# Softmax weights turned on VectorE in four batches of the last cross attention and two of the last self attention, the context staged through the output buffer, and a shorter look-ahead for keys

## The chip, the cores and the metric

The kernel runs on one core of a Trainium2 chip, in fp32. The metric is the device time of one execution in microseconds (us), smaller is better: 1604.43 us is the median of three runs (1602.59 to 1607.76). About 0.3% (5 us) is what a measurement of this kernel can tell from no change.

The engines by the profile's names: PE (matrix multiply; PEld is its weight load), DVE (VectorE), ACT (ScalarE), POOL (GpSimd) and SP (the queue from which nearly all DMAs are issued, in the order of the program).

## The reference, cut to what matters

Four transformer blocks follow each other on x of 8 batches x 112 rows x 256 columns. All of them read the same context of 8 x 375 x 192. Every attention has 16 heads, of 64 columns in blocks L0, L1 and L2 and of 16 in block L3.

```python
x = self_attn(ln(x)) + x ; x = cross_attn(ln(x), ctx) + x ; x = geglu_ff(ln(x)) + x    # L0: stages 0, 1, 2
x = self_attn(ln(x)) + x ; x = cross_attn(ln(x), ctx) + x ; x = geglu_ff(ln(x)) + x    # L1: stages 3, 4, 5
x = x + cross_attn(ln(x), ctx)                                                         # L2: stage 6
x = x + causal_self_attn(ln(x)) ; x = x + cross_attn(ln(x), ctx) ; x = x + mlp(ln(x))  # L3: stages 7, 8, 9
# attention: w = softmax(q k^T / sqrt(dh)) over keys; out = w v; per batch and head 112 x 112 or 112 x 375 weights
```

## The kernel before, in words

All of x, the normalised and transposed input `hT`, the transposed context (`ctxA`, `ctxB`) and the attention output `oT` ([128, 8, 896], the "output buffer") stay in SBUF. Queries, keys and values live in one `arena`; weight matrices pass through a ring `wpool` of six slots, rows of biases through a ring of two.

Attention is cut into 176 *steps* (`add_step`): one batch with 8 heads in a self attention (2 steps a batch), one batch with 4 heads in a cross attention (4 steps a batch). The steps of stage 7 are woven between those of stages 6 and 8 (dictionary `after`). I number steps from 0 in that order: stage 6 begins at step 96, stage 8 at step 138, its batch 4 at step 158. A step has these parts.

- S (`emit_s`): the scores q k^T on PE (L1079) into PSUM, then the softmax. With 64-column heads DVE finds the row maxima (L1030), ACT takes exp with a row sum (L1036), POOL multiplies by the reciprocal (L1043). With 16-column heads (stages 7 and 8) one DVE operation adds the mask, negates, writes the masked scores to SBUF and leaves the maximum (L1012), ACT takes exp (L1020), and the division is done later on the output (`emit_norm`, `emit_scale`).
- The weights must then stand with keys on partitions. There are two ways. An *unturned* step transposes each 112 x 128 block on PE (T, L1109) and DVE or ACT copies four at a time out of PSUM (L1116, L1119, L355). A *turned* step transposes 32 x 32 blocks on DVE (`flip`, L1057), writes four strips to DRAM (`send`, L1063) and reads them back in the final layout (`fetch`, L980): the bounce through DRAM exchanges the 32-row strips. Two write tiles and two read tiles in `stage` serve all turned steps in turn; the fetch of a step waits for the PV of the turned step two before it.
- PV (`emit_pv`, L1142): weights times values on PE; the result is copied into `oT`.

`TURN(st, b, g)` says which steps are turned: in stage 7 batches 0 to 4, in stage 8 none, in stages 0, 1, 3, 4 and 6 nearly all.

Everything else is an `Item` with a cost, a due time in steps (`deadline`) and what it needs: query, key and value projections (L715, L756, L833/L842, L867/L876, L908/L917), output products with the next layer norm (L681), transposes of the normalised rows (L649) and of the context (L939), feed-forward. A planner (`Plan`) emits the program once: the loop over steps at the end of the kernel places S up to `lead(s)` steps ahead of PV (two, or up to four where turned steps follow each other) and fills in items by due time. Keys and values of a cross attention are *jobs*, opened by `open_jobs` when their due time is within a limit; before, the limit is `i + 1.5 + lead(...)`, so 3.5 to 5.5 steps after step i. Items that make queries, keys or values in the pending list are held back until `ahead` = 7 steps before they are due. The order so made is fixed; at run time each engine and the SP queue go through their own part of it in order.

The context is read by three loads into the weight ring (`add_ctx`: batches 0 to 2, 3 to 5, 6 and 7) and transposed on PE batch by batch (`add_context_transposes`, L939); batches 2 to 7 are due during stage 1, one every four steps. Each transposed batch needs one more DMA (`ctxB` to `ctxB`).

```python
fetches.append((s, dram))                                  # send: four DMAs stage -> DRAM, then
while fetches and turned[fetches[0][0]] < emptied[0] + 2 and free_of(fetches[0][0]): ...   # fetch: one DMA back
plan.open_jobs(1 if i + 1 >= first_of(8, 0) or i + 2 in woven else 2, i + 1.5 + lead(min(nxt, hi - 1)), seg)
```

## Time and profile before

| what | value |
|---|---|
| median of three runs | 1604.43 us |
| the profiled execution: its time / span of its instructions | 1604.4 us / 1602.6 us |
| PE, DVE, ACT, POOL busy | 95%, 55%, 45%, 34% of the span |
| granted TensorE clock | 0.985 |
| DMA moved, mean rate | 212.49 MB, 133 GB/s |
| sends and fetches | 488 and 122 DMAs, for 122 turned steps |
| stage 8 begins (scores of step 138) / its batch 4 (step 158) | 1372.9 us / 1469.6 us |

The page lists busy time by engine; since matmuls are pipelined and their ends are modelled, a busy PE is not PE at its peak. How fast PE takes matmuls is read from where they start. The list of windows gives busy time of all engines, the granted clock and DMA for a stretch; the chain of waits follows the work that ended last back in time.

### The profile page before, as it was taken

The page shows a single profiled execution, that of the slowest core. Times are in us where ns is not written, and L with a number is a line of the kernel's source. Part 1 is how long each engine was busy: PE and PEld are TensorE (multiplying, and loading weights), DVE is VectorE, ACT ScalarE, POOL GpSimd, SP SyncE. Part 2 cuts the span into 40 slices and gives each one's busy share as a digit, 9 for nine tenths or more (in the row PEclk, how much of TensorE's full clock was granted, in tenths as well). Part 3 has the DMA queues.
Part 4 walks back from the last instruction along what each step waited for, and adds up shares of the span by engine and source line. Part 5 has one row for each costly group of instructions (what it writes and reads, how often), then busy time and mean ns, then how long its engine had stood idle before and what let it go on. Part 6 is the DMA issues. An engine that isn't in the chain of part 4 may idle for free.

```text
span 1602.6 us, 28310 instructions
## 1 busy us (share of the span) xinstructions
PE 1530.4 (95%) x10452; PEld 1035.4 (65%) x10452; DVE 886.4 (55%) x2029; ACT 723.4 (45%) x2359; POOL 537.2 (34%) x787
## 2 busy tenths in 40 slices
PE   9998999999999989999999999989999997999999
PEld 8776656665567876666565556655566545666667
DVE  3664555566442265565655542455656766577762
ACT  3452435444332444444443351234445545587772
POOL 1333434444320223354334230433434336212210
PEclk9999999999999999999999999999999999899999
DMA  6165464766601056556575712045467667300000
GB/s 179 39 206 153 140 215 149 236 188 177 191 30 53 24 145 198 145 158 213 172 204 158 208 46 77 2 125 178 159 194 197 189 178 222 126 2 2 2 2 23
DMA packets 128305, 212.49 MB, mean 133 GB/s; under 512 B 11287, under 2 KB 112295, under 8 KB 128167
## 3 DMA queue, kind: packets, MB, share of 16 engines
q1 hardware_dynamic: 127927, 210.52, 44.5%
q8 instruction: 82, 1.34, 0.3%
q14 instruction: 56, 0.46, 0.1%
q10 hardware_dynamic: 240, 0.17, 0.0%
HBM read 122.45 MB, written 87.43 MB: 131 GB/s over the span
## 4 chain that ended last, share of the span: by engine, by line
PE 73%; DVE 9%; ACT 6%; DMA 5%; issue 3%; POOL 3%; SPq 1%; DVEq 0%; ACTq 0%; POOLq 0%
PE mm L681 12%; PE mm L715 10%; PE s L1079 8%; PE mm L1142 8%; PE mm L867 6%; PE mm L833 6%; PE mm L1384 6%; PE mm L842 4%; PE mm L876 4%; DVE stage L1057 3%; ACT pr L1036 3%; DMA stage<-b 3%; PE mm L1109 2%; DMA b<-stage 2%; POOL pr L1043 2%
## 5 line engine op out<-in xcount | busy, mean ns | idle before, releaser
L1043 POOL TENSOR_TENSOR pr<-pr,rinv 128x750 f32<-128x750 f32 (+3 forms) x224 | 327.7, 1474 | 342.6 <-DVE rinv L1041 342.0
L1036 ACT ACTIVATE pr<-s,nm 128x375 f32<-128x375 f32 (+3 forms) x640 | 302.3, 493 | 268.6 <-DVE nm L1030 213.5
L1057 DVE STREAM_TRANSPOSE stage<-pr 128x768 f32<-128x768 f32 (+2 forms) x218 | 206.9, 970 | 71.3 <-POOL pr L1043 62.7
L1079 PE MATMUL s<-arena 64*128 64x375 f32 (+6 forms) x1792 | 218.9, 403 | 16.4 <-ACT pr L1036 8.0
L1030 DVE TENSOR_REDUCE nm<-s 128x2 f32<-128x750 f32 (+3 forms) x224 | 205.6, 949 | 33.9 <-PE s L1079 32.2
L355 ACT COPY arena<-mm 128x375 f32<-128x375 f32 (+5 forms) x186 | 96.5, 520 | 274.8 <-PE mm L842 125.9
L1142 PE MATMUL mm<-stage,arena 128*64 128x112 f32 (+5 forms) x3840 | 189.9, 268 | 16.9 <-DMA stage<-b 11.5
L1142 PEld LDWEIGHTS mm<-stage,arena 128*64 128x64 f32 (+5 forms) x3840 | 168.8, 134 | 55.7 <-issue 18.9
L363 DVE COPY arena<-mm 128x375 f32<-128x375 f32 (+5 forms) x186 | 109.1, 594 | 158.9 <-PE mm L876 71.2
L1079 PEld LDWEIGHTS s<-arena 64*128 64x128 f32 (+3 forms) x1792 | 122.8, 184 | 101.3 <-issue 33.5
L1020 ACT ACTIVATE pr<-pr,nm 112x375 f32<-112x375 f32 (+2 forms) x256 | 124.7, 492 | 26.9 <-DVE nm L1012 26.7
L1036 ACT ACTIVATION_READ_ACCUMULATOR pr<-s,nm 128x1 f32 (+1 forms) x640 | 135.4, 212 | 0.0
L611 POOL TENSOR_TENSOR rs<-ve,mhalf 128x1 f32<-128x1 f32 x70 | 39.5, 564 | 212.1 <-DVE ve L609 212.0
L1041 DVE RECIPROCAL rinv<-sums 128x2 f32<-128x2 f32 (+3 forms) x224 | 37.6, 168 | 127.7 <-ACT pr L1036 127.1
L1002 POOL MEMSET pr<- 128x9 f32 (+1 forms) x218 | 23.0, 108 | 233.5 <-DVE stage L1057 205.3
L833 PE MATMUL mm<-ctxA,L_xattn_Wk 128*128 128x375 f32 x256 | 92.3, 488 | 6.4 <-ACT arena L351 2.5
L867 PE MATMUL mm<-L_xattn_Wv,ctxA 128*128 128x512 f32 (+1 forms) x192 | 93.7, 615 | 0.9 <-DVE x L685 0.5
L715 PE MATMUL mm<-hT,L_xattn_Wq 128*128 128x224 f32 x384 | 82.7, 361 | 4.2 <-DVE arena L363 2.1
L1109 PEld LDWEIGHTS mm<-ident,pr 112*128 112x128 f32 (+2 forms) x600 | 66.8, 151 | 30.3 <-issue 14.2
L1109 PE MATMUL mm<-ident,pr 112*128 112x112 f32 (+2 forms) x600 | 78.9, 266 | 4.3 <-ACT pr L1020 3.1
L685 DVE TENSOR_TENSOR x<-mm,x 128x256 f32<-128x256 f32 x70 | 29.4, 420 | 94.9 <-PE mm L681 94.3
L681 PE MATMUL mm<-L_xattn_Wo,oT 128*128 128x256 f32 x336 | 79.3, 391 | 0.8 <-ACT oT L355 0.8
(138 smaller groups left out, 2252.1 us busy)
## 6 DMA issues: line engine op xcount, KB each, us to landing
b<-stage SPq DMA_DIRECT2D x344, 192.0 KB, 3.9
stage<-b SPq DMA_DIRECT2D x86, 768.0 KB, 5.9
b<-stage SPq DMA_DIRECT2D x144, 128.0 KB, 3.6
stage<-b SPq DMA_DIRECT2D x36, 512.0 KB, 4.6
L_xattn_Wo<-in_L_xattn_Wo_dram SPq DMA_DIRECT2D x3, 1024.0 KB, 14.9
L_xattn_w_ff<-in_L_xattn_w_ff_dram SPq DMA_DIRECT2D x3, 1024.0 KB, 6.7
L_xattn_Wv<-in_L_xattn_Wv_dram SPq DMA_DIRECT2D x4, 512.0 KB, 7.3
L_xattn_Wq<-in_L_xattn_Wq_dram SPq DMA_DIRECT2D x2, 1024.0 KB
```

Source lines behind the costliest of these rows:

```text
L681: nc.tensor.matmul(ps[:, :D], lhsT=oT[:, c, t * P : (t + 1) * P], rhs=got[wv or w][:, c, :], start=(c == 0), stop=(c == n - 1),)
L715: nc.tensor.matmul(ps[:, i * 2 * T : (i + 1) * 2 * T], lhsT=got[w][:, k, m * P : (m + 1) * P], rhs=hT[:, k, lo:hi], start=(k == 0), stop=( ...
L833: nc.tensor.matmul(ps[:, :S], lhsT=got[wv][:, (2 * u + i) * P : (2 * u + i + 1) * P], rhs=ctxA[:, cols], start=True, stop=False,)
L867: nc.tensor.matmul(ps[: KCH[c][1], :], lhsT=lhs(ctxA, slice(0, KA), c), rhs=got[w][:, hf * 512 : (hf + 1) * 512], start=True, stop=False,)
L1020: return nc.scalar.activation(pr, pr, AF.Exp, bias=nm, scale=-1.0, accum_out=bsums[(st, b)][:, h : h + 1])
L1030: nc.vector.tensor_reduce(nm[:, :, :ns], sv, AX.X, ALU.max, negate=True)
L1036: nc.scalar.activation(pr[:, bk, sl, :], sv[:, bk, sl, :], AF.Exp, bias=nm[:, bk, sl : sl + 1], accum_out=sums[:, bk, sl : sl + 1],)
L1043: nc.gpsimd.tensor_tensor(pr, pr, rinv[:, :, :ns].unsqueeze(3).to_broadcast([rows, 2, ns, nk]), ALU.mult)
L1057: nc.vector.transpose(dst, src)
L1079: nc.tensor.matmul(tiles[i][:, n % 2, (n // 2) * nk : (n // 2 + 1) * nk], lhsT=qap(h), rhs=kap(h), start=True, stop=True,)
L1109: nc.tensor.transpose(pt[:kl, m * T : (m + 1) * T], cell[h][:, c * P : c * P + kl], ident[:T, :T])
L1142: nc.tensor.matmul(po[p0 : p0 + dp, blk * T : (blk + 1) * T], lhsT=got[vk][:kl, hv * dp : (hv + 1) * dp], rhs=wt, start=(c == 0 and par(h) ...
```

## The change

- Stage 8 becomes a turned stage: batches 0 to 3 turn their weights on DVE (16 steps); its queries are laid out in 32-row strips, and its due times move two steps earlier, as for the other turned stages.
- Stage 7: batches 5 and 6 are turned too (four steps), so 0 to 6 are.
- The context: batches 0 to 2 still go through the weight ring, in one load of 9 chunks; the other 15 chunks are loaded into columns 448 to 831 of `oT` by two DMAs that need no ring slot. All eight batches are due in stage 0 (3.5 + b/2). The PVs of steps 8 and 9 (batch 4 of stage 0, the first to write the part of `oT` with context in it) are placed after all context transposes.
- Key and value jobs are opened when due within 2.5 steps, instead of 3.5 to 5.5; `ahead` is 6 instead of 7.
- The mask of the context is kept on 128 partitions instead of 112, for turned steps.

Counted in the two programs: 224 transposes (L1109) fewer on PE; 56 copies of them out of PSUM fewer (35 on ACT, 21 on DVE); 40 DVE transposes more (32 of 128 x 768, 8 of 128 x 512); 80 sends and 20 fetches more on SP (64 and 16 of a cross step, 16 and 4 of a self step); 40 small memsets more on POOL for the columns that pad the weights, and 8 for the gaps in the queries. The number of exps, maxima, scores and PVs stays.

```diff
--- before.py
+++ after.py
@@ -27,7 +27,7 @@
 NQ, QR = 4, 28
 LEAD = 4
 TAIL = 6
-TURNED = (0, 1, 3, 4, 6, 7)
+TURNED = (0, 1, 3, 4, 6, 7, 8)
 NWT = 8
 NEG = -1.0e30
 EPS = 1e-5
@@ -95,7 +95,7 @@
         self.pool = {r: deque() for r in rings}
         self.refs, self.maker, self.ev = {}, {}, {}
         self.pending, self.loads, self.jobs, self.opened = [], deque(), [], []
-        self.now, self.step, self.ahead = 0.0, 0, 7
+        self.now, self.step, self.ahead = 0.0, 0, 6
 
     def add(self, it, filler=True):
         self.items[it.key] = it
@@ -500,13 +500,17 @@
         key = ("w", "ctx", i)
 
         def fn():
-            t = wpool.tile([CH, len(bs) * 3, DC], F32, tag="w", name="cn")
-            nc.sync.dma_start(
-                t, a["ctx_768"][bs[0] : bs[-1] + 1].rearrange("b (c p) d -> p (b c) d", p=CH)
-            )
-            got[key] = t
-
-        plan.add_load(Item(("load", key), 0, fn, makes=[key]))
+            src = a["ctx_768"].rearrange("b (c p) d -> p (b c) d", p=CH)
+            if i:
+                nc.sync.dma_start(oT[:CH, :, 448:640], src[:, 9:17, :])
+                nc.sync.dma_start(oT[:CH, 0:7, 640:832], src[:, 17:24, :])
+                got[("c", i)] = lambda n: oT[:CH, (n - 9) % 8, 448 + 192 * ((n - 9) // 8) :][:, :DC]
+                return
+            t = wpool.tile([CH, 9, DC], F32, tag="w", name="cn")
+            nc.sync.dma_start(t, src[:, 0:9, :])
+            got[("c", i)] = lambda n: t[:, n, :]
+
+        plan.add_load(Item(("load", key), 0, fn, makes=[] if i else [key]))
 
     def add_last_self(key, name):
 
@@ -581,14 +585,14 @@
         key = ("w", "cm")
 
         def place():
-            got[key] = wpool.tile([T, B, S], BF16, tag="w", name="cm")
+            got[key] = wpool.tile([P, B, S], BF16, tag="w", name="cm")
 
         plan.add_load(Item(("load", key), 0, place, makes=[key]))
         for b in range(B):
 
             def ctx_mask(b=b):
                 c = B * T + b * S
-                nc.gpsimd.tensor_scalar_mul(got[key][:, b, :], got[src][:T, c : c + S], NEG)
+                nc.gpsimd.tensor_scalar_mul(got[key][:, b, :], got[src][:, c : c + S], NEG)
 
             plan.add(Item(("mask", b), 0, ctx_mask, first_of(7, 0) - 6 + 0.5 * b, uses=[src, key], seg=SEG[6]))
 
@@ -928,22 +932,22 @@
 
     def add_context_transposes(deadline):
         for b in range(B):
-            key = ("w", "ctx", b // 3)
-
-            def fn(b=b, key=key):
-                cn = got[key]
+            key = ("w", "ctx", int(b > 2))
+
+            def fn(b=b):
+                cn = got[("c", int(b > 2))]
                 cols = slice(b * S, (b + 1) * S)
                 for k0, kl, dst in ((0, KA, ctxA), (KA, KB, ctxB)):
                     pc = mm_tile()
                     for c in range(3):
                         nc.tensor.transpose(
                             pc[:kl, c * CH : (c + 1) * CH],
-                            cn[:, (b % 3) * 3 + c, k0 : k0 + kl], ident[:CH, :CH],
+                            cn(3 * b + c)[:, k0 : k0 + kl], ident[:CH, :CH],
                         )
                     evac(dst[:kl, cols], pc[:kl, :S], S)
                 nc.sync.dma_start(ctxB[KB:, cols], ctxB[:KB, cols])
 
-            plan.add(Item(("ctxT", b), 0.7, fn, deadline(b), uses=[key], deps=[(("S", 2 + b // 3), 2.0)] + [(("ctxT", c), 1.5) for c in range(b - 1, b) if b]))
+            plan.add(Item(("ctxT", b), 0.7, fn, deadline(b), uses=[] if b > 2 else [key], deps=[(("S", 2 + b // 3), 2.0), (("load", key), 14.0)] + [(("ctxT", c), 1.5) for c in range(b - 1, b) if b]))
 
 
 
@@ -1172,7 +1176,8 @@
             )
         plan.add(
             Item(("PV", s), 0.193 * nch * len(heads) / par + 0.25, emit_pv, uses=uv,
-                 deps=[(("S", s), 0)] if turn else [(("T", s, i), 0) for i in range(len(banks))]), False
+                 deps=([(("S", s), 0)] if turn else [(("T", s, i), 0) for i in range(len(banks))])
+                 + ([(("ctxT", c), 0) for c in range(B)] if (st, b) == (0, 4) else [])), False
         )
         steps.append(0 if turn else len(banks))
         if last:
@@ -1255,7 +1260,7 @@
             km = lambda h: h // 8
             vt = lambda h, c, b=b: (("v", st, b, 0, c), h)
             opos = lambda h: (32 * (h // 2 % 4), 0)
-            tail = (lambda b=b: got[("w", "cm")][:, b, :], opos, g // 2, g == 3, (st, b, g // 2))
+            tail = (lambda b=b: got[("w", "cm")][: P if turn else T, b, :], opos, g // 2, g == 3, (st, b, g // 2))
         heads = [h for blk in blocks for h in blk]
 
         def qap(h, j=j, tb=tb, qu=qu):
@@ -1315,7 +1320,7 @@
         return {
             0: b > 1, 1: (b > 0 or g > 1 or 0 in TURNED) and b < B - 1, 3: b > 0,
             4: (b > 0 or g > 1 or 3 in TURNED) and b < B - 1,
-            6: (b, g) > (0, 1) and b < (B if 7 in TURNED else 4), 7: b < 5,
+            6: (b, g) > (0, 1) and b < (B if 7 in TURNED else 4), 7: b < B - 1, 8: b < 4,
         }[st]
 
     for i, part in enumerate(order):
@@ -1520,11 +1525,10 @@
             plan.add_load(Item(("load", "x", 4), 0, lambda: load_x(nc.sync, 4, 5, 6)))
             add_row(("row", s0), n[4])
             add_brows()
-            add_ctx(0, [0, 1, 2])
+            add_ctx(0, None)
         add_w(w(n[3]), n[3])
         if bi == 0:
-            add_ctx(1, [3, 4, 5])
-            add_ctx(2, [6, 7])
+            add_ctx(1, None)
         add_w(w(n[7]), n[7])
         add_ctx_w(w(n[8]), n[8], True)
         add_ctx_w(w(n[9]), n[9], False)
@@ -1541,7 +1545,7 @@
         add_products(s0, s1, w(n[3]), 8, after_pv(s0), norm_by(s1))
         add_norm_transposes(s1, n[12], n[13], hT_by(s1))
         if bi == 0:
-            add_context_transposes(lambda b: f1 + 4 * b - 3 - LEAD if b > 1 else 7 + b)
+            add_context_transposes(lambda b: 3.5 + 0.5 * b)
         cross_stage(s1, w(n[7]), w(n[8]), w(n[9]), 0.125, None)
         add_products(s1, s2, w(n[10]), 8, after_pv(s1), norm_by(s2))
         add_norm_transposes(s2, n[17], n[18], hT_by(s2))
@@ -1668,7 +1672,7 @@
             fetch()
 
 
-            plan.open_jobs(1 if i + 1 >= first_of(8, 0) or i + 2 in woven else 2, i + 1.5 + lead(min(nxt, hi - 1)), seg)
+            plan.open_jobs(1 if i + 1 >= first_of(8, 0) or i + 2 in woven else 2, i + 2.5, seg)
     plan.step = len(steps)
     while plan.pending:
         plan.drain(plan.pending[0].key)
```

## The prediction

> **What bounds the kernel now.** I read the page first, then busy time by stretches cut at the starts of stages and batches, then the chain of waits, then the costs of single operations.
>
> The page (busy time, forty slices):
>
> ```profile
> PE 1530.4 (95%) x10452; PEld 1035.4 (65%) x10452; DVE 886.4 (55%) x2029; ACT 723.4 (45%) x2359; POOL 537.2 (34%) x787
> PE   9998999999999989999999999989999997999999
> DVE  3664555566442265565655542455656766577762
> DMA  6165464766601056556575712045467667300000
> ```
>
> PE looks full everywhere. It isn't: a transpose lasts 266 ns in the list of groups, but twelve follow each other in 1.34 us (chain below), 0.11 us each. If each matmul is counted by its start-to-start time in runs of its form (0.096 us a transpose, 0.216 a 256-column pass, 0.43 a 512-column pass), PE takes in work for about 1398 of the 1602.6 us; 200 us are waits and half clock. They lie unevenly, and the lists of windows show where (us; PE, PEld, DVE, ACT, POOL busy; clock; DMA share; GB/s):
>
> ```profile
> 121.60:126.40 4.80, 0.24 (x6) 0.03 (x2) 2.84 (x4) 4.31 (x27) 1.19 (x1) 1.00 1.09 274
> 126.40:133.20 6.80, 6.40 (x27) 5.26 (x28) 1.32 (x3) 1.18 (x8) 2.22 (x3) 0.50 0.94 253
> ...
> 1288.20:1372.90 84.70, 68.94 (x522) 46.07 (x518) 50.30 (x152) 36.46 (x134) 41.69 (x67) 0.88 0.68 208
> 1372.90:1403.40 30.50, 29.16 (x316) 21.76 (x316) 22.68 (x98) 22.30 (x74) 9.03 (x14) 1.00 0.20 68
> 1403.40:1469.60 66.20, 62.81 (x707) 43.20 (x706) 52.23 (x196) 52.12 (x169) 13.95 (x24) 1.00 0.01 2
> ```
>
> Three things: near 121.6 PE stands still for 5 us with the DMA engines full, then runs at half clock for 6.8 us. From 1288 to 1373 (end of stage 6, stage 7, all turned) the matmuls' own time is 52 of 84.7 us. From 1403 to 1470 (steps 144 to 157: 12 cross steps of stage 8, 2 self steps, none turned) DMA idles, DVE and ACT are at 79%, a step takes 66.2/14 = 4.73 us, of which 51/14 = 3.6 us are matmul time.
>
> The chain of waits, in order of time (start, us, what):
>
> ```profile
> 118.86 7.80 DMA stage<-b
> ...
> 1355.86 3.91 DMA b<-stage
> 1359.85 6.62 DMA stage<-b
> 1366.51 2.51 PE mm L1142 x24
> ...
> 1457.59 1.34 PE mm L1109 x12
> 1459.45 1.30 ACT pr L1020 x4
> ```
>
> The first wait is PV for a fetch. Before stage 8 the round trip through DRAM carries the chain; in stage 8 transposes on PE alternate with exps on ACT.
>
> Groups by form, from 1400 us on (first two lines) and from 1150 to 1400 (the others):
>
> ```profile
> L1012 DVE CUSTOM_DVE_ANT_0 pr<-s,cm 112x375 f32<-112x375 f32 x112 | 54.8, 543 | 6.2 <-PE s L1079 4.9 <-ACT pr L1020 1.0
> L1116 DVE COPY stage<-mm 128x448 f32<-128x448 f32 x28 | 17.4, 620 | 7.5 <-PE mm L1109 7.2
> ...
> L1057 DVE STREAM_TRANSPOSE stage<-pr 128x768 f32<-128x768 f32 x38 | 35.3, 958 | 0.4
> L1057 DVE STREAM_TRANSPOSE stage<-pr 128x512 f32<-128x512 f32 x20 | 12.8, 684 | 0.0
> ```
>
> and DMA issues (KB each, us to landing):
>
> ```profile
> b<-stage SPq DMA_DIRECT2D x344, 192.0 KB, 3.9
> stage<-b SPq DMA_DIRECT2D x86, 768.0 KB, 5.9
> ```
>
> **The change part by part.** The sum is made against the profiled execution, 1604.4 us (1.8 us outside its span); the median is 1604.43, so nothing is added between them.
>
> *1. The transposes taken off PE, steps 138 to 157.* 224 x 0.096 to 0.112 us = 21.5 to 25 us of PE time. On the same steps DVE gains 32 x 0.958 + 8 x 0.684 = 36.1 us and loses 21 copies x 0.62 = 13 us; ACT loses 35 x 0.53 = 18.5 us and takes over some 5 us of evictions from DVE. Whether PE's time comes out depends on what else paces a step. Three bounds for steps 138 to 157 (16 cross, 4 self; 1372.9 to the last PV of step 157 at 1474.5, 101.6 us now):
> - DVE. Busy now 22.7 + 52.2 + about 3.5 (to 1474.5) = 78.4 us; + 36 - 13 - 5 = 96.5 us. Counted by start-to-start times (a transpose 0.90 us, a copy 0.54, a maximum 0.47) it is 91.5. So DVE, idle for 22% of the stretch today, fills 90 to 95% of it: the stretch cannot fall below 91.5 us, 10 us of gain at most.
> - The round trip. In order, PE does PV(s), items, S(s+3), S(s+4); the maxima of S(s+4) precede the flips of s+4 on DVE; then 4 sends, the fetch, PV(s+4). From the end of flips to a landed fetch, when nothing blocks SP, rows of before give 9.0 to 9.9 us (1192.8 to 1201.9; 1281.7 to 1290.7). Add PV 0.6, items and scores between PV and the next S 4.5, maxima 1.9, flips 1.8: 18 to 19 us per 4 steps, 4.5 to 4.8 us a step.
> - DMA. A cross step moves 2 x 786 KB, a self step 2 x 524 KB: 29.4 MB, and the two feed-forward matrices of stage 9 (2.1 MB), loaded from 1368 us on today, now stand in SP's queue between the sends of steps 138 and 139. 31.5 MB in 100 us is 315 GB/s. The fullest slice of the page has 236, though 328 GB/s occur for 8 us.
>
> Three resources at 80 to 95% whose waits do not coincide: I take 5.2 us a step, 104.5 us, so **+3**. Low end -10 (DVE's floor). High end: the pace of the present turned stretch with the same mixture of cross and self steps, steps 124 to 137, 1257.8 to 1354.5 us = 7.44 us a step, or 149 us: +47. I stay near the floor because those 64-column steps also hold a POOL multiply (1.44 us twice) and a DVE maximum twice as long (0.93 us against 2 x 0.47), and more PE work.
>
> What is queued behind what: SP blocks at a fetch until PV two steps back is done (SP waited 120 us for PE that way), and sends behind it wait too; with self pairs the first send of the next cross step stands ahead of the second self fetch, so this waits for that cross step's flip, as at 1344 to 1350 today. POOL's 40 memsets (0.11 us each) and the wider mask cost nothing: POOL is busy 14 of 66 us there; were it not, 4.4 us.
>
> A rule speaks against this part: the Trainium skill, "VectorE: DVE Perf Modes", section "Rules for kernel authors", tells authors to transpose 128 x 128 on TensorE where PSUM is an acceptable destination. The row first: twelve transposes cost PE 1.34 us and three copies of 0.53 to 0.62 us on ACT and DVE; turning costs DVE 1.92 us and five DMAs. By the rule alone this part would be a loss of DVE's extra 18.5 us; by the rows it is what the fullest of three resources makes of it.
>
> *2. Context and first weights early, stage 0.* The wait at 121.6 (5.0 us) is for the fetch of step 11, which shares the DMA engines with a third context load and the query weights of stage 1. In the changed order the whole context and these weights are issued before the first send, and PV of steps 10 and 11 stands about 31 us of matmul time after its scores instead of 19 to 24. The wait goes, and with it the half clock: 6.8 us at 0.50 = 3.4 us. Bounds: -8.4; and +2, if the eight context transposes (16 copies x 0.54 us) crowd DVE and ACT in stage 0, where ACT is busy about half the time. I take **-8**. The transposes only change place: 3.7 us of matmuls move from stage 1 to stage 0. 16 ring-free context chunks shift no later load that PE waits for in this trace.
>
> The Trainium skill, "TensorE: Matmul & The Clock Gate", section "What's actually happening", says that an idle window of about 3.4 us drops the clock to half. This case agrees at 126.4, but also shows 0.50 from 1191.4 to 1198.2 after waits of 1.8 us at most, so shorter waits cost too; by the page alone only the 3.4 us here would be at stake.
>
> *3. Keys and values opened later.* Less work stands ahead of stage 6, batch 4: the order has 5.1 us less matmul time between S of step 96 and S of step 112, a stretch at 95% PE; it reappears after step 112, where 148 us of matmuls spread over 205 us, so it falls into waits. Also PV of steps 134 to 137 stands 20, 19, 20 and 16 us of matmuls after its scores instead of 19, 14, 14 and 11, where the round trip now leaves gaps of 4.9 and 1.8 us. Against it: at steps 120 to 127 that distance shrinks by up to 4.5 us, and stage 3 and 4 orders shift both ways by a few us. Bounds -9 and +4, value **-5**.
>
> *4. The rest* (steps 158 to the end, 133 us now) keeps its kind of work; 109 us of matmuls before, 110 after: 0, within 2 us.
>
> Sum: 1604.4 + 3 - 8 - 5 = **1594.4 us**.
>
> **The rivals.**
> - *PE's time comes out whole*: part 1 at -21 with DVE ahead of need, 1604.4 - 21 - 8 - 5 = 1570. For it: the tables show PE at 95%. Against: DVE's floor allows 10 of these 21 in the stretch, the rest only if stage 9's items move forward.
> - *The round trip paces the last cross attention* (the slower side). Place: SP's queue and the two read tiles, steps 138 to 157; the price is 20 x (pace) - 101.6. At 5.73 us a step the 13 us of parts 2 and 3 are used up; from 6.0 on the kernel is slower by over 5 us. At 6.3 it gives 1604.4 - 13 + 24.4 = 1616. For it: 7.44 us a step in the stretch just before; 315 GB/s wanted. Against: DVE and POOL work per step is smaller there.
> - *Washed out*: the pace ends near 5.7, within 5 us (0.3%) of before; the gain of part 2 pays for part 1.
>
> **How the numbers follow.** My forecast 0.47 (own range 1584 to 1600), PE's time whole 0.13 (1562 to 1580), round trip 0.28 (1609 to 1635), washed out 0.12. Faster by over 0.3%: 0.42 of the first and all of the second, 0.55; within: the rest of the first and the washed out, 0.17; slower: 0.28. The range leaves out one in ten each side: 1572 to 1621.
>
> **What would show each step.** Part 1: in the windows of stage 8, DVE at 90% or more and DMA share near 0.8 for batches 0 to 3; chain there of flips, b<-stage and stage<-b in place of L1109 and exps; about 5.2 us a step. Part 2: no wait of PE for stage<-b before 150 us, and full clock there. Part 3: the scores of step 138 begin some 13 us earlier than 1372.9. I am wrong if step 138 starts no earlier, if steps 138 to 157 take over 115 us, or if DVE stays below 85% there while PE still waits for fetches.

## The result, and the profile after

The changed kernel takes 1619.11 us (median of 4 runs, 1618.09 to 1621.23), the kernel before beside it 1603.51 us (1601.14 to 1607.76): a ratio of 1.0096, 95% interval 1.0071 to 1.0121. It is slower by 1%; the forecast was 1594 us and faster.

The busy time and the slices of the page of the changed kernel:

```profile
PE 1529.6 (94%) x10228; PEld 1021.6 (63%) x10228; DVE 889.7 (55%) x2020; ACT 723.0 (45%) x2368; POOL 540.9 (33%) x835
PE   9999999999999989999999999999999977777999
DVE  3656556565331565655656433555666756666752
PEclk9999999999999999999999999989999987778999
DMA  6275565676301266456577211254777866776000
```

The hole in PE's row in the fourth slice is gone. A new one has opened in slices 33 to 37, where the clock falls too. The starts of the score matmuls of single steps, before and after, say when the time came and went: step 23 starts 14.3 us earlier than before, step 64 18.8, step 112 18.9, step 130 26.0 and step 138 32.9 us earlier (1340.0 for 1372.9). From there the lead melts: 19.2 us at step 144, 12.3 at step 150, and step 158 starts 14.3 us later than before. So 33 us are won ahead of the last cross attention and 47 lost in it (11 of both are only the earlier scores of a turned step, as e1_no_turn below shows). The lists of windows of the changed kernel and, last, of the kernel before for the same steps 138 to 157 (us; PE, PEld, DVE, ACT, POOL busy; clock; DMA share; GB/s):

```profile
0.00:146.60 146.60, 141.79 (x990) 114.65 (x992) 78.64 (x151) 64.67 (x295) 45.05 (x77) 1.00 0.53 148
1340.00:1489.10 149.10, 108.79 (x941) 68.10 (x942) 96.49 (x322) 73.00 (x248) 29.22 (x89) 0.78 0.75 227
```

```profile
1372.90:1474.70 101.80, 97.08 (x1099) 68.17 (x1099) 79.92 (x312) 77.92 (x253) 23.62 (x40) 1.00 0.06 22
```

A step there takes 149.1/20 = 7.46 us where it took 5.09. This measure begins with the scores of step 138, so it holds their earlier start too; from the last PV of step 137 to that of step 157 pass 127.3 us where 95.5 did, 6.37 us a step instead of 4.78. No engine is full: VectorE is busy for 65% of the stretch, PE for 73% at a mean clock of 0.78. The chain of waits names what PE waits for (start, us, what):

```profile
1397.56 4.94 DMA stage<-b
1402.54 0.97 PE mm L1146 x16
...
1416.28 5.00 DMA stage<-b
1421.28 1.29 DVE stage L1061 x2
1423.64 2.47 PE s L1083 x8
...
1467.43 3.06 DMA b<-stage
1470.57 6.27 DMA stage<-b
```

Fetches (`stage<-b`), flips (L1061) and sends (`b<-stage`) carry it, in place of the transposes and exps of before. The waits in 1340 to 1489 us, of SP's queue and of PE (us in total, times, longest):

```profile
SPq L1067 <- DVE stage L1061: 42.9, 14, 6.8
SPq L984 <- DMA b<-stage: 26.6, 21, 4.3
```

```profile
PE mm L1146 <- DMA stage<-b: 21.1, 8, 6.3
PE s L1083 <- DVE nm L1016: 17.9, 10, 3.8
```

PE waits both for fetched weights (ahead of PV) and for VectorE to empty a score tile (ahead of the scores); SP waits for flips. It is a ring of engines that wait for one another, and the experiments had to find where it can be opened.

### The profile page after: what moved, and what is told of

The parts are those of the page before. It is cut to its first block, busy times and chain, and to the rows that moved or that the text cites. A ratio compares the mean times of both kernels' runs of the same rounds, so it can differ in the third digit from the quotient of the medians.

```text
span 1619.4 us, 28108 instructions
## 1 busy us (share of the span) xinstructions
PE 1529.6 (94%) x10228; PEld 1021.6 (63%) x10228; DVE 889.7 (55%) x2020; ACT 723.0 (45%) x2368; POOL 540.9 (33%) x835
## 4 chain that ended last, share of the span: by engine, by line
PE 76%; DVE 7%; ACT 6%; DMA 5%; issue 4%; POOL 2%; SPq 1%; DVEq 0%; ACTq 0%; POOLq 0%
PE mm L685 12%; PE mm L719 10%; PE mm L1146 9%; PE s L1083 9%; PE mm L837 7%; PE mm L871 7%; PE mm L880 4%; PE mm L846 4%; PE mm L1389 4%; ACT pr L1040 3%; DMA stage<-b 3%; PE mm L796 3%; DVE stage L1061 3%; DMA b<-stage 2%; PE mm L1113 2%
## 5 line engine op out<-in xcount | busy, mean ns | idle before, releaser
L1061 DVE STREAM_TRANSPOSE stage<-pr 128x768 f32<-128x768 f32 (+2 forms) x258 | 240.3, 957 | 38.7 <-POOL pr L1047 27.7
L1083 PE MATMUL s<-arena 64*128 64x375 f32 (+7 forms) x1792 | 232.0, 414 | 29.8 <-DVE nm L1016 18.5
L355 ACT COPY arena<-mm 128x375 f32<-128x375 f32 (+4 forms) x201 | 102.9, 518 | 281.2 <-PE mm L880 122.0
L1146 PEld LDWEIGHTS mm<-stage,arena 128*64 128x64 f32 (+5 forms) x3840 | 168.3, 135 | 69.6 <-issue 26.9
L1083 PEld LDWEIGHTS s<-arena 64*128 64x128 f32 (+3 forms) x1792 | 127.3, 188 | 122.8 <-issue 30.1
L363 DVE COPY arena<-mm 128x375 f32<-128x375 f32 (+5 forms) x171 | 99.7, 593 | 161.9 <-PE mm L880 87.1
L1024 ACT ACTIVATE pr<-pr,nm 128x112 f32<-128x112 f32 (+3 forms) x256 | 124.3, 489 | 53.5 <-DVE nm L1016 45.1
L1006 POOL MEMSET pr<- 128x9 f32 (+1 forms) x258 | 26.4, 107 | 260.6 <-DVE stage L1061 230.1
L689 DVE TENSOR_TENSOR x<-mm,x 128x256 f32<-128x256 f32 x70 | 29.4, 422 | 110.7 <-PE mm L685 110.4
L719 PEld LDWEIGHTS mm<-hT,L_xattn_Wq 128*128 128x128 f32 x384 | 70.5, 191 | 13.7 <-issue 4.1
L685 PEld LDWEIGHTS mm<-L_xattn_Wo,oT 128*128 128x128 f32 x336 | 62.3, 190 | 15.5 <-issue 5.7
## 6 DMA issues: line engine op xcount, KB each, us to landing
L_xattn_Wq<-in_L_xattn_Wq_dram SPq DMA_DIRECT2D x2, 1024.0 KB, 10.8
```

The lines of the kernel that those rows point to most:

```text
L355: nc.scalar.copy(dst, src)
L685: nc.tensor.matmul(ps[:, :D], lhsT=oT[:, c, t * P : (t + 1) * P], rhs=got[wv or w][:, c, :], start=(c == 0), stop=(c == n - 1),)
L719: nc.tensor.matmul(ps[:, i * 2 * T : (i + 1) * 2 * T], lhsT=got[w][:, k, m * P : (m + 1) * P], rhs=hT[:, k, lo:hi], start=(k == 0), stop=( ...
L1024: return nc.scalar.activation(pr, pr, AF.Exp, bias=nm, scale=-1.0, accum_out=bsums[(st, b)][:, h : h + 1])
L1061: nc.vector.transpose(dst, src)
L1083: nc.tensor.matmul(tiles[i][:, n % 2, (n // 2) * nk : (n // 2 + 1) * nk], lhsT=qap(h), rhs=kap(h), start=True, stop=True,)
```

## Experiments

Step 138 to the last PV of step 157 is called the stretch. It starts at 1340.0 in the changed kernel; all stretches below are read from the starts of scores and the ends of PV in the traces. A kernel that issues the scores of step 138 earlier has a longer stretch by that alone, so device times and the time between the last PVs of steps 137 and 157 are set beside it where it matters.

**The parts one by one.** First the change without its turned weights, the turned weights alone, and each of the other two parts alone.

```
e1_no_turn, from the changed kernel
-TURNED = (0, 1, 3, 4, 6, 7, 8)
+TURNED = (0, 1, 3, 4, 6, 7)
-    7: b < B - 1, 8: b < 4,
+    7: b < 5,
     (and the wide context mask back to T rows)
e2_turn_only: the same lines the other way, in the kernel before
e3_ctx_only: e1_no_turn with "self.ahead = 7" and "i + 1.5 + lead(min(nxt, hi - 1))" as before
e4_jobs_only: the kernel before with "self.ahead = 6" and "i + 2.5"
```

> The changed kernel with the weights of stage 8 (and self batches 5, 6) on the old path again, transposed by PE; early context and later keys stay. Theory A (all of the loss is the turned stage 8, the rest of the change is worth the 33 us by which step 138 started earlier): step 138 starts near 1340, steps 138 to 157 take 100 to 103 us again instead of 148.8, the time is 1571 (1565 to 1578). Rival (later keys push work and waits into stage 8, whoever turns the weights): steps 138 to 157 take over 115 us here too, the time is 1587 or more.

> The kernel before with the turned stage 8 and nothing else. Theory A: steps 138 to 157 take 145 to 152 us instead of 101.6, step 138 starts at 1373 as before, the time is 1651 (1643 to 1658). Rival (the turned steps are slow only because keys and values come later): they take about 105 us, the time is 1600 to 1612.

> The kernel before with the early context and first weights alone. Theory A, with the trace of the changed kernel, in which the lead grows to 14 us by step 23 and 19 us by step 64: most of that is the context's, the time is 1588 (1584 to 1594). By the prediction's own figure (8 us) it is 1596; if the lead before step 64 is the later keys' instead, it is 1600 or more.

> The kernel before with keys and values opened at 2.5 steps ahead (and the shorter look-ahead of the pace) alone. Theory A: it is worth the 14 us that step 138 gained after step 64 (19 to 33), the time is 1590 (1585 to 1595). By the prediction's own figure (5 us) it is 1599; if early context and late keys only help together, it is 1604.

| kernel | us | ratio to before | 95% interval | stretch, us |
|---|---|---|---|---|
| e1_no_turn | 1584.54 | 0.9886 | 0.9860 to 0.9912 | 101.8 |
| e2_turn_only | 1643.52 | 1.0250 | 1.0217 to 1.0283 | 147.7 |
| e3_ctx_only | 1597.48 | 0.9964 | 0.9948 to 0.9980 | 101.8 |
| e4_jobs_only | 1588.84 | 0.9910 | 0.9877 to 0.9942 | 103.8 |

Turned weights cost 34.6 us on top of the other parts (1619.1 against 1584.5) and 40.7 us alone; the stretch is 149 or 148 us long wherever they are turned and 102 to 104 where not. So neither later keys nor early context make the loss. The early context is worth 5.3 us against the 1602.78 us of before in this comparison, later keys 13.9, both 18.2. That is less than the 33 us of lead at step 138, from which 1571 us had been expected of e1_no_turn, because 11.4 us of that lead were no gain: in e1_no_turn step 138 starts at 1351.4. The code issues the scores of a turned step up to four steps ahead of PV, those of others two steps, so that turning step 138 moves its scores ahead of other work. e1_no_turn is faster than both kernels. Its stretch, from the list of windows:

```profile
1351.40:1453.20 101.80, 94.84 (x1091) 66.33 (x1091) 76.97 (x303) 79.99 (x259) 21.21 (x38) 1.00 0.04 13
```

**Which turned steps.** The turned self batches 5 and 6 alone (`7: b < B - 1`, stage 8 not turned), and the cross steps alone (`7: b < 5, 8: b < 4`).

> Self batches 5 and 6 turned, the last cross attention not; context early, keys later. If the loss belongs to the turned cross steps (16 of 20), this is within 5 us of e1_no_turn: 1580 to 1590. Rival: two turned self steps between unturned cross steps make PE wait for a trip that nothing covers (24 us or more from scores to PV at a lead of two), 5 to 8 us each pair: 1594 to 1601.

> The changed kernel with self batches 5 and 6 on the old path and the 16 cross steps turned. If the costs add (34.6 us in all, 18 of them shown for the four self steps alone): 1601. If any turned step in this stretch sets the slow pace: 1613 to 1620.

e12_self_only takes 1602.44 us (0.9983, 0.9964 to 1.0002), its stretch 119.4 us, 17.6 longer than that of e1_no_turn: four turned steps of 20 lose nearly all of the 18.2 us that the rest had won. The rival held, a little above its range. e15_cross_only takes 1626.01 us (1.0132, 1.0083 to 1.0181), its stretch 156.9 us: worse than with the self steps turned too, against both expectations. What PE waits for in the two stretches, first e12_self_only, then e15_cross_only:

```profile
PE mm L1146 <- DMA stage<-b: 10.7, 3, 4.4
```

```profile
PE mm L1146 <- DMA stage<-b: 36.9, 9, 10.5
```

Each passage between turned and unturned steps leaves a trip that nothing covers, with single waits up to 10.5 us. By the code this is `lead`: it gives a turned step only three steps of lead where the step two back is not turned. That reason was only read from the code, not tried.

**One leg of the trip at a time.** Four changed kernels, each with one suspect taken away in steps 138 to 157.

```
e5_half_bytes
+    n = width[s] if s < 138 else width[s] // 2
     send:  w_tile(s)[32 * i : 32 * i + 32, :, :n]      fetch: d_tile(s)[:, :, :n]
e6_dummies, ahead of the scores and of PV
+    if turn and s >= 138: warm(6)
e7_flip_now
-    turn_until(s)
+    turn_until(s + 1 if s >= 138 else s)
e8_lead6
-    while n < LEAD and ...
+    while n < (6 if s >= 138 else LEAD) and ...        (bounce: bufs=6)
```

> The changed kernel, but steps 138 to 157 send and fetch only the first half of each row of turned weights (so half of the weights that PV reads there are old ones: part of the computation is left out). Theory B, bytes set the pace (the DMA engines are 82% busy there): steps 138 to 157 fall from 149 us to 110 or less, the time to 1580 or less. Theory A, the length of the round trip sets it (24 to 35 us from scores to PV, of which sends and fetch are some 11 us, over 4 steps in flight): shorter transfers save 2 to 3 us of the trip, 0.6 us a step, 137 us, 1607.

> The changed kernel with six 128-column matmuls that nobody reads, some 0.7 us, ahead of the scores and of PV of each of the steps 138 to 157 (27 us more of PE work at full clock), to keep PE from resting. Theory C, the half clock that follows PE's waits is what makes the trip long (68 us at 0.50 among these 149): the clock holds, and steps 138 to 157 take 130 us or less, the time is 1600 or less. Theory A (the trip's other legs): the half clock is a consequence, the steps take 145 to 165 us, the time is 1616 to 1635.

> The changed kernel with the flips of steps 138 to 157 directly behind the step's own maxima in VectorE's order, not behind the next step's maxima and the evictions between. Theory A, the flip's place in the order is the long leg (in step 150 the exps are done at 1425.4, the flip comes at 1432.7): the trip loses 6 to 8 us, 1.5 to 2 us a step, 149 becomes 110 to 119 us, the time 1580 to 1589. Rival: VectorE now waits for ScalarE's four exps (2.4 us) in each step with all evictions behind it, and nothing is gained: 1615 or more.

> The changed kernel with the scores of steps 138 to 157 up to six steps ahead of PV in place of four (and six DRAM buffers in place of four). Theory A, a trip of given length shared by the steps in flight: 149 us becomes 105 to 120, the time 1577 to 1592. Rival D, the rings (four probability tiles, two write tiles and two read tiles, each for two steps) hold the number in flight where it is: 145 to 152 us, 1616 to 1622.

The legs of a step's trip, mean of the 20 steps, from matching each step's records in the trace (us). The trace marks the landing of a transfer in 16 parts, and a transfer counts here as landed with the last of them: PV of step 143 starts at 1402.54, 0.04 us after the last part of its fetch. "Send" is from the first send's issue to the last one's landing, "to fetch" from there to the fetch's issue, and the total runs from the end of the scores to the first PV matmul. The flips themselves (1.7 us; 3.0 in e5, 2.1 in e14 and e16) and up to 1.2 us from their end to the first send make up the rest. The rows of the later kernels are used further down:

| kernel | time | ratio to before (95%) | stretch | scores to flip | send | to fetch | fetch | to PV | total |
|---|---|---|---|---|---|---|---|---|---|
| changed kernel | 1619.1 | 1.0096 (1.0071 to 1.0121) | 149.1 | 12.4 | 6.3 | 1.0 | 5.4 | 2.0 | 29.5 |
| e5_half_bytes | 1597.1 | 0.9930 (0.9904 to 0.9957) | 128.1 | 7.8 | 5.0 | 2.0 | 3.9 | 2.3 | 24.3 |
| e6_dummies | 1627.3 | 1.0127 (1.0064 to 1.0190) | 158.2 | 12.9 | 5.8 | 1.7 | 5.5 | 4.3 | 32.5 |
| e7_flip_now | 1618.3 | 1.0078 (1.0047 to 1.0109) | 148.5 | 9.7 | 5.7 | 5.5 | 6.4 | 0.8 | 29.8 |
| e8_lead6 | 1625.0 | 1.0112 (1.0082 to 1.0143) | 152.8 | 11.8 | 6.0 | 11.4 | 6.4 | 2.4 | 39.9 |
| e13_dve_in_order | 1607.2 | 1.0018 (1.0007 to 1.0030) | 136.1 | 9.5 | 7.1 | 0.7 | 5.7 | 0.9 | 26.8 |
| e14_dve_in_order_flip_now | 1609.2 | 1.0036 (1.0017 to 1.0056) | 139.3 | 4.4 | 6.5 | 5.6 | 6.4 | 1.4 | 26.9 |
| e16_fetch_first | 1607.2 | 1.0028 (1.0012 to 1.0044) | 144.5 | 5.9 | 7.2 | 2.2 | 5.9 | 4.0 | 28.4 |
| e17_in_order_half_bytes | 1589.3 | 0.9912 (0.9883 to 0.9942) | 121.0 | 7.9 | 5.2 | 1.6 | 4.2 | 2.3 | 22.9 |

*Half the bytes* give 21 us of the stretch back, between the two expectations (128 us; 137 and 110 had been named). The two transfers themselves get only 2.7 us shorter; the leg from scores to flip falls by 4.6 us though nothing was done to it, and the whole trip by 5.2. So bytes do not set the pace by themselves (the DMA share falls to 0.55 and the stretch still needs 128 us), but a shorter transfer is paid back about twice. The waits fit a ring in which VectorE waits for PE and PE for the fetch. In e5_half_bytes they are, for 42.9 and 21.1 us in the changed kernel:

```profile
SPq L1068 <- DVE stage L1061: 31.9, 13, 6.0
```

```profile
PE mm L1147 <- DMA stage<-b: 13.5, 5, 4.6
```

*Dummies* kept the clock at 0.95 and the stretch became 9 us longer. Its window, and the group of the dummy matmuls (busy us, mean ns, idle time ahead):

```profile
1337.50:1495.70 158.20, 148.00 (x1410) 113.28 (x1409) 96.81 (x322) 73.14 (x248) 28.90 (x89) 0.95 0.72 211
```

```profile
L389 PE MATMUL mm<-ident 128*128 128x128 f32 x473 | 65.5, 290 | 0.0
```

PE took 65.5 us of extra matmuls for 9 us of time, so its own work does not fill the stretch, and the 130 us of theory C did not come. That the half clock is only a consequence of the waits is likely by this, but not shown: the dose had been put at 27 us and was 65.5, PE is now busy for 148.0 of 158.2 us, and a gain from the held clock may be hidden behind the dummies.

*Six steps ahead* made the trip ten us longer and no step faster: the weights lie ready in DRAM for 11.4 us. In each of the steps 140 to 157 the read tile came free, with the end of PV two steps back, only after the weights had landed, 9.0 us on the mean. The number of steps in flight is set by the tiles, not by the lead (rival D, whose ranges were passed by 1 and 3 us). *Flips at once* changed nothing, as their rival had it: they took 2.7 us off the first leg, and the wait ahead of the fetch grew by 4.5 us: it is issued 3.2 us after the later of two things, the landing of the sends and the end of PV two steps back, where that was 0.8 us in the changed kernel.

**Other orders of the sends.** Since in e7_flip_now the fetch was late behind other sends, three kernels gave the sends another place.

```
e9_flip_now_act_sends: e7_flip_now, and
-    nc.sync.dma_start(dram[:, :, i, :]...
+    (nc.scalar if s >= 138 else nc.sync).dma_start(dram[:, :, i, :]...
e10_flip_now_lead6_late_sends: e7_flip_now + e8_lead6, and
-    while sends and not (turns and ...):
+    while sends and not (turns and ...) and (sends[0][0] < 138 or sends[0][0] <= nxt - 3):
e11_flip_now_lead6_act_sends: e9_flip_now_act_sends + e8_lead6
```

> Early flips as in e7_flip_now, and the sends of steps 138 to 157 issued from ScalarE's queue, so that SP holds fetches only. Theory F, SP's single order is the loop (in e7_flip_now the data has landed 2 us before PV two steps back has ended, but the fetch is issued 4.3 us after that PV, behind sends that wait for flips): the fetch follows the later of the two by 1 us or less, some 3 us per pair of steps come out, steps 138 to 157 take 115 to 128 us and the time is 1584 to 1598. Rival G: the delay only moves, to ScalarE's exps that now stand behind the sends' waits and to VectorE behind them; 140 us or more, 1610 or more.

> Early flips, six steps ahead, and each send emitted only when the scores two steps later are out, so that on SP a fetch never stands behind a send whose flip is still to come; all on SP. Theory F: the time that SP waits for flips (47 to 61 us in the other runs) falls below 15 us, the steps take 110 to 125 us, 1580 to 1595. Rival G (the read tiles' own loop, PV, fetch of 5 us, PV's place in PE's order, sets 7.4 us a step whatever SP does): 140 us or more, 1610 or more.

> Early flips, six steps ahead, sends from ScalarE's queue. Theory F: the least of the three, 105 to 120 us, 1575 to 1590. Rival G: as e8_lead6, 145 to 155 us, 1615 to 1625.

In the last two, flips of the step two later are emitted ahead of some sends, so these carry another step's weights (a changed computation), and wait for the later flip. All are slower than the changed kernel: 1642.33 us (1.0232, 1.0187 to 1.0277), 1630.19 us (1.0157, 1.0112 to 1.0202) and 1657.24 us (1.0325, 1.0274 to 1.0377). On ScalarE's queue the sends hold up exps, as rival G had it (in e9, between 1340 and 1485 us, ScalarE stands idle ahead of exps for 23.5 us that the profile puts down to issuing, and for 12.7 us behind a send). In e10 SP waited even longer for flips (50.9 us, in 1340 to 1485), those of the step two later; so it did not test what it was made for, and says nothing on SP's order.

**VectorE's order.** The timeline of VectorE in the changed kernel, around the flips of step 148 (the first line of L1061), 149 (the second) and 150 (the last); the scores of step 150 had ended at 1418.8:

```profile
1419.92 0.42 DVE L689 TENSOR_TENSOR x<-mm,x 128x256 f32<-128x256 f32 x1 [2.40 <-PE mm L685]
...
1421.27 1.30 DVE L1061 STREAM_TRANSPOSE stage<-pr 128x512 f32<-128x512 f32 x2
1422.50 0.51 DVE L1016 CUSTOM_DVE_ANT_0 pr<-s,cm 128x375 f32<-128x375 f32 x1
...
1424.35 1.30 DVE L1061 STREAM_TRANSPOSE stage<-pr 128x512 f32<-128x512 f32 x2
...
1428.57 0.27 DVE L1159 COPY oT<-mm 128x112 f32<-128x112 f32 x1 [1.07 <-PE mm L1146]
1431.17 0.76 DVE L817 TENSOR_TENSOR arena<-mm,ctx_w 128x256 f32<-128x256 f32 x2 [2.33 <-PE mm L921]
1432.39 0.39 DVE L1204 TENSOR_TENSOR oT<-mm,oT 128x224 f32<-128x224 f32 x1 [0.46 <-PE mm L1195]
1432.70 1.82 DVE L1061 STREAM_TRANSPOSE stage<-pr 128x768 f32<-128x768 f32 x2
```

The code emits the flips of a step right behind the next step's maxima. The scheduler has put evictions between the maxima of step 151 and the flips of step 150: an output copy, value products and a scaling, each of which waits for PE, while PE waits for fetches. The exps of step 150 ended at 1425.6, its flips began at 1432.7. e13 pins VectorE's instructions of the stretch to the emitted order, e14 does so with the flips directly behind the step's own maxima, and e16 also puts the two fetches of a pair ahead of the next pair's sends on SP.

```
e13_dve_in_order: called ahead of PV of step 157; "pinned" holds where step 138 begins
+    ins = [i for i in nc.cur_bb.bb.instructions[pinned[0] :] if i.engine == nc.vector.engine]
+    for p, i in zip(ins, ins[1:]):
+        tc.add_manual_dep(i, p.name, <order only, no wait for p to finish>)
e14_dve_in_order_flip_now: e13_dve_in_order + e7_flip_now
e16_fetch_first: e14_dve_in_order_flip_now, and a send of step s >= 138 is held while fetches of s - 2 or older are due
```

> The changed kernel with VectorE's instructions of steps 138 to 157 held in the order in which the code emits them: maxima of the next step, flips, and only then the evictions (the scheduler had put evictions of PE's items ahead of many flips). Theory H, the flips' place behind evictions that wait for PE is the loop's long leg (scores to flip 12.4 us on the mean): the leg falls to 7 us, steps 138 to 157 from 149 to 120 to 132 us, the time to 1590 to 1602. Rival G (the trip's other waits take over, as in e7_flip_now): 143 us or more, 1612 or more.

> The same, with the flips directly behind the step's own maxima. Theory H: scores to flip 5 us or less, 115 to 128 us, 1585 to 1597. Rival G: SP's order takes over, with the fetch issued 4 us after PV two steps back: 143 us or more, 1612 or more.

> As e14_dve_in_order_flip_now, and on SP the two fetches of a pair of steps ahead of the sends of the next pair. Theory F and H together (two in-order queues, VectorE and SP, each carry a step's trip behind a later step's wait): PE's waits for fetches fall from 21 us to under 10, 105 to 120 us, 1575 to 1590. Rival G: 140 us or more, 1609 or more.

They take 1607.15, 1609.17 and 1607.24 us (ratios and legs in the table above). The order of VectorE alone is worth 12 us of the time and 13 of the stretch, about half of what theory H had expected. Then something else closes the ring. Waits of e13 in its stretch, of SP's queue, VectorE and PE:

```profile
SPq L1076 <- DVE oT L1217: 13.8, 3, 7.6
...
SPq L1076 <- DVE stage L1070: 6.5, 5, 3.0
```

```profile
DVE stage L1070 <- DMA b<-stage: 20.8, 6, 5.9
```

```profile
PE mm L1159 <- DMA stage<-b: 25.2, 10, 7.0
PE s L1094 <- DVE nm L1025: 4.0, 8, 0.7
```

SP's sends wait for VectorE, for flips and for what it does ahead of them, 29.4 us over all such lines instead of 47.7, PE for score tiles 4.0 instead of 17.9; but flips now wait 20.8 us (4.4 before) for the sends of two steps back to leave the write tile, and PE's wait for fetches has grown to 25.2. In e14 and e16 the first leg falls to 4.4 and 5.9 us, and other legs take it back; in e16 the fetch follows the later of landed sends and freed read tile by 0.1 us on the mean, so SP's order alone is not what is left. Is what is left the transfers?

> VectorE in emitted order as in e13_dve_in_order and half the bytes as in e5_half_bytes (half of the turned weights that PV reads are old ones: part of the computation is left out). If the two causes are different legs and add (13 and 24 us): steps 138 to 157 take 105 to 116 us, the time is 1575 to 1588. If the halved bytes had helped only by loosening VectorE's lockstep: 125 to 132 us, 1596 to 1604.

e13 with half the bytes takes 1589.34 us. The windows of the stretch, e5_half_bytes and then e17:

```profile
1336.60:1464.70 128.10, 102.75 (x941) 64.32 (x942) 95.00 (x322) 72.64 (x249) 28.96 (x89) 0.82 0.55 149
```

```profile
1340.90:1461.90 121.00, 100.04 (x941) 62.50 (x942) 95.42 (x323) 72.34 (x248) 29.48 (x89) 0.84 0.58 159
```

Order and bytes are worth 13 and 21 us alone and 28 together: they overlap by 6 us, and the result lies between the two expectations. The stretch is still 19 us longer than that of e1_no_turn, but it starts 10.5 us earlier. Between the last PVs of steps 137 and 157 it takes 100.5 us, where e1_no_turn takes 96.7 and the changed kernel 127.3, and in device time e17 is 4.8 us slower than e1_no_turn. So, as far as a run with half of the weights left out can say it, VectorE's order and the bytes of the transfers account together for some 30 of the 34.6 us that the turned weights cost. The last 5 were not settled; the clock is still at 0.84.

**The same order elsewhere.** e18_no_turn_in_order is e1_no_turn with VectorE pinned in steps 112 to 137, where both kernels turn 64-column steps.

> e1_no_turn (early context, later keys, stage 8 not turned) with VectorE in emitted order in steps 112 to 137, where stage 6 and self batches 0 to 4 are turned. If flips behind evictions cost there what they cost in steps 138 to 157 (0.65 us a step): 17 us less over 26 steps where PE has no slack, 1568 to 1575. Rival: the emitted order puts the second maximum of a 64-column step behind a reciprocal that waits for ScalarE's exps, 1 us or more a step: 1584 to 1610.

1607.93 us (1.0016, 0.9995 to 1.0036), 23 us slower than e1_no_turn; steps 112 to 137 take 230.2 us for 203.4. The rival held: there the emitted order puts the second maximum behind a reciprocal that waits for ScalarE's exps. These waits in the two windows, first e18, then e1_no_turn:

```profile
DVE rinv L1054 <- ACT pr L1049: 53.7, 32, 7.0
```

```profile
DVE rinv L1045 <- ACT pr L1040: 19.5, 27, 0.9
```

The scheduler's order is the better one in one kind of step and the worse one in the other.

## Why the prediction was wrong

*Part 1 failed, in its pace.* "I take 5.2 us a step": by the forecast's own measure, from the scores of step 138 to the last PV of step 157, it was 7.46, so the term +3 was +47. In device time the turned weights cost 34.6 us (e1_no_turn), because 11.4 of the 47 are scores that only start earlier. That +47 is also the high end that was named and set aside is luck: its 7.44 us a step run from scores to scores (1257.8 to 1354.5 us, 13 steps), and counted so the stretch has 6.46 (1340.0 to 1462.8 us, 19 steps). The pieces of the failed term:

- VectorE: forecast 96.5 us of work in these steps, measured 96.49. The sum of durations was right and the bound drawn from it did not bind: the engine was busy for 65%, not 90 to 95%.
- The trip: "18 to 19 us per 4 steps". From the start of the scores to PV alone it took 31 us (1.5 + 29.5). PE takes the steps in pairs: behind PV of steps s and s + 1 come the scores of s + 6 and s + 7, not of s + 3 and s + 4, and from PV to PV six steps later pass 37.2 us on the mean, 6.2 us a step. The flips, set behind "maxima 1.9", began 12.4 us behind the scores: the four exps (2.4 us) and the next step's maxima had been left out of the sum, and the flips stood behind evictions that wait for PE (e13: 13 us of the stretch). From flips to a landed fetch, forecast 9.0 to 9.9 us, it took 13.4 (0.7 + 6.3 + 1.0 + 5.4). The two rows behind the forecast were from times when SP was free, and they were read to the first of the 16 parts of a landing; to the last (1203.6 and 1292.4 us) they are 10.8 and 10.7 us.
- The combination. Three resources at 80 to 95% were taken as if a step cost little more than the fullest of them. They are links of one ring: PE waits for a fetch, VectorE for PE, SP for VectorE. Time lost in one link is lost in the others (e5: 2.7 us of shorter transfers took 5.2 us off the trip).
- The reason for setting 7.44 us aside was that those 64-column steps hold more work of POOL, VectorE and PE. (Not in the maxima: one of 0.93 us serves two heads, as 2 x 0.47 do.) Counted between last PVs, steps 124 to 137 of the kernel before take 6.88 us each and the stretch 6.37. The lighter steps were faster by 0.5 us, not by the 2.2 that the forecast gave them.

The rival *the round trip paces the last cross attention* is what happened. Its formula gives 47.6 with the measured 7.46, and its example, 6.3 us a step and 24.4 us, was below the 34.6 of device time too. Its 1616 us lie near the measured 1619.1 partly by luck: parts 2 and 3 brought 18.2 us where 13 had been put. *PE's time comes out whole* fell: PE did lose its transposes, and waits and half clock filled their place.

*Part 2 held, somewhat smaller:* -8 forecast, -5.3 in e3_ctx_only. The wait at 121 us and the half clock behind it are gone: the first window has clock 1.00 up to 146.6 us, and PE's waits for fetches up to 150 us come to 0.3. The lead grows to 11.4 us at step 23 and is given back in part, to 5.3 at step 138.

*Part 3 held in direction and was mis-sized:* -5 forecast, bounds -9 and +4, -13.9 in e4_jobs_only. It was costed in stages 6 and 7 alone, and there it was about right: in the trace of e4_jobs_only the lead grows by 6.3 us between steps 96 and 138 (13.2 to 19.5). The rest is ahead of that, 6.5 us by step 23 and 9.7 between steps 48 and 64, in stage 3, which the forecast had put down as shifts "both ways by a few us". Why later keys help in stage 3 was not tried.

Step 138 started 32.9 us early instead of 13, and of the signs named for being wrong two came: steps 138 to 157 took over 115 us, and VectorE stayed below 85% while PE waited for fetches. The rule of the Trainium skill, "VectorE: DVE Perf Modes", section "Rules for kernel authors", to transpose 128 x 128 on TensorE where PSUM can be the destination, agrees with e1_no_turn: undoing the turn is worth 34.6 us here. (VectorE's extra work, which the forecast puts at 18.5 us in this place, is 18.1 by its own terms: 36.1 - 13 - 5.)

## What to carry to other kernels

Where several in-order queues pass one item round, ask for the length of the whole trip and for what stands ahead of each hand-over in each queue; busy shares below 100% on all of them do not mean that the time is near the fullest one's. A measured pace of the same ring elsewhere in the same trace was the better estimate here (6.88 us a step between PVs for 6.37, where the sum of durations had 5.2), if both are read between the same marks. Read a transfer to its last part: what waits for it waits for that. Before an off-loaded step is costed, look at the order that the scheduler really issues: an eviction ahead of a hand-over ties the producer to its own consumer.

## What was not expected of the hardware

The clock dropped to 0.50 again and again after short waits, as the prediction had seen once. One place in the changed kernel: a wait of 3.75 us ended at 1423.6 and was followed by half clock until 1430.4. Then, at full clock, the longest wait was one of 1.66 us, ended at 1435.5, and the clock dropped again at 1437.3. (The next wait, of 1.68 us, came behind that drop.) The windows:

```profile
1430.00:1437.30 7.30, 5.61 (x36) 2.36 (x36) 5.67 (x16) 2.21 (x7) 0.61 (x3) 0.97 0.38 95
1437.30:1444.10 6.80, 5.12 (x41) 3.45 (x40) 4.90 (x16) 2.73 (x10) 0.52 (x3) 0.50 1.00 290
```

PE was idle for 1.7 us of the first 7.3 and went to half clock for the next 6.8. The Trainium skill, "TensorE: Matmul & The Clock Gate", section "What's actually happening", speaks of an idle window of about 3.4 us; by these rows a shorter pause goes with the drop too, and the measured ones decide here. What exactly trips the clock was not tried.
